# One raise for a chunk's twelve transposes and four activations, and a PSUM bank freed by its reader alone

## The chip, the cores and the metric

The program runs on one core of a Trainium2 chip. A core has five engines that run side by side, each an in-order queue: TensorE (PE in the profile, its weight loads PEld), VectorE (DVE), ScalarE (ACT), GpSimd (POOL) and SyncE (SP). They meet through semaphores: an instruction may wait until a semaphore has reached a value, and may raise one when it is done. DMA transfers raise semaphores when they land. The metric is the device time of one execution in microseconds; the median of 10 runs before is 7348.97 us (7343.96 to 7355.32).

## The reference

Two layers are applied to x, which has 4 images of 128 channels and 128 by 128 points.

```
x = x + deformable_conv(ln_c(x), w_off, w_conv)     # layer 0
t = tokens(x);  t = t + moe(ln_t(t))                # 8 experts, the best 2
x = x + fourier_mix(ln_c(x), alphas, betas)         # layer 1
t = tokens(x);  t = t + expert_choice(ln_t(t))      # 64 experts, 8 tokens each
```

The deformable convolution takes nine taps. For each tap and each output point a small convolution gives an offset; the input is read there by bilinear interpolation, which is a weighted sum of four neighbours; the nine samples of all channels go through w_conv. It is this sampling that the change touches: 4 images x 128 rows x 9 taps, each a gather of 128 points with four neighbours of 128 channels.

## The kernel before

**Tables and gathers.** Each image's normalised input is written to a table in DRAM whose entry holds two neighbouring rows' channels, so that one gathered stretch holds the four neighbours of a point. A *chunk* is one image row and three taps; there are 4 x 128 x 3 = 1536 chunks. Four rows make a group, and a group has twelve chunks: four rows with taps 0 to 2 (k0 = 0), then with 3 to 5, then with 6 to 8.

**A chunk's way** (class Chunk):

- `gather` (POOL): three indirect DMAs fill a tile g of 128 points x 3 taps x 4 neighbours x 128 channels. Seven such tiles are in turn (AHEAD), so the gather for chunk n + 7 reuses the tile of chunk n and waits until PE has read it.
- `weighted` (DVE): one multiplication with the interpolation weights, over all three taps when k0 = 0, over two taps otherwise.
- `weighted_too` (ACT), for k0 > 0: the third tap's four neighbours, one activation each, with the weight as its scale.
- `summed` (PE): a PSUM bank named trg; for each tap four transposes, one per neighbour, accumulate into the same 128 x 128, which sums the neighbours and turns channels to partitions. Twelve transposes in all.
- `moved` (ACT): one copy sT of the bank to SBUF. After the fourth row `convolved` multiplies sT with w_conv into the bank `sums` (PE).

**Everything else** is cut into coroutines (padding, offsets, block, mixed, experts, the last layer's Experts and Ending) that are resumed slot by slot. A slot is one chunk. The loop at the end of the function writes the order by hand: weighted of chunk n + 1, moved of chunk n - 2, one step of every coroutine, weighted_too of n + 1, summed of n, and then as many banks of the coroutines as there is room for (`Turns.fills`). `InOrder` keeps every engine's instructions in this order. Reading a bank comes two slots after its filling (`turns.hop` = 2).

**PSUM banks.** `bank` hands out six banks in turn (BANKS); two more are `sums` and `spread`. Fillings are groups of matmuls: four transposes (tr), one or four matmuls (pe, ps, pq, pl, po) or more. Readers are mostly one ACT copy of the whole bank; the experts' bank pe is read by one addition, or by four DVE instructions of a quarter each.

**Semaphores** are not written by hand. The framework records which instruction touches which tile and makes waits of it: a bank's new filling waits for all that touched its last content, thus for its readers and for PE's own earlier matmuls; a reader waits for the matmuls; a writer to g waits for the transposes. An instruction has room for one wait; what it needs beyond that goes into separate wait instructions ahead of it. Raises that nobody needs are folded into a later instruction of the same engine where the framework can do so: in the trace, 1,153 chunks have one raise on the twelfth transpose alone, and 383 chunks have five, on transposes 8 to 12, where transposes 9 to 12 each wait for one of the four activations.

All instructions are issued through the helper at line 101, so the profile shows L101 everywhere, and groups are told apart by their tiles.

Of the kernel before, what the change touches and what calls it, by code (L numbers as in the profile page):

```python
# [42 lines left out]
F32 = mybir.dt.float32  # L43
I32 = mybir.dt.int32
U32 = mybir.dt.uint32
AF = mybir.ActivationFunctionType
ALU = mybir.AluOpType
AX = mybir.AxisListType
PSUM = bass.MemoryType.PSUM
# [19 lines left out]
CB = 16  # L69
# [21 lines left out]
class InOrder:  # L91


    def __init__(self, tc, engine):
        self.tc, self.engine = tc, engine

    def __getattr__(self, name):
        issue = getattr(self.engine, name)

        def issued(*args, **kwargs):  # L100
            return self.tc.keep_in_program_order(issue(*args, **kwargs))  # L101

        return issued


class Engines:
    def __init__(self, tc):
        nc = tc.nc
        self.tensor, self.vector = InOrder(tc, nc.tensor), InOrder(tc, nc.vector)
        self.scalar, self.gpsimd = InOrder(tc, nc.scalar), InOrder(tc, nc.gpsimd)  # L110
        self.sync = InOrder(tc, nc.sync)


# [73 lines left out]
def metaformer_kernel(  # L187
# [16 lines left out]
    nc = tc.nc  # L204
# [6 lines left out]
    ident = const.tile([P, P], F32, name="ident")  # L211
# [26 lines left out]
    with ExitStack() as main:  # L238
# [7 lines left out]
        p_x = main.enter_context(tc.tile_pool(name="p_x", bufs=BANKS, space=PSUM))  # L246
# [2 lines left out]

        def bank(shape, name):  # L250

            return p_x.tile(shape, F32, name=name, tag="bank")

        eng = Engines(tc)
        turns = Turns()
# [4 lines left out]
        class Image:  # L260


            def __init__(self, b):
                self.b = b
                self.table = tabs.tile([TW * TC, 2 * P], F32, name=f"table{b}", tag="table")
                self.grid = self.table.rearrange("(i j) e -> i j e", j=TC)
                self.index = pw.tile([P, P, TAPS], I32, name=f"index{b}", tag="index")
                self.weight = {}
                self.xc = {}
                self.z = {}  # L270
                self.tails = {}


                self.read = self.normed = self.continued = self.sent = 0
                self.offsets = self.placed = self.known = 0
                self.left = 0
                self.direct = P // RB
                self.rooms = {}
# [91 lines left out]
        by = wts.tile([P, CB, TAPS], F32, name="by")  # L370
# [43 lines left out]
        def transposes(src, n, by=None):  # L414

            tr = bank([P, n, P], "tr")
            for i in range(n):
                if by is None:
                    eng.tensor.transpose(tr[:, i, :], src(i), ident)
                else:  # L420
                    eng.tensor.matmul(
                        tr[:, i, :], lhsT=src(i), rhs=by, is_transpose=True, start=True, stop=True
                    )
            return tr


# [2 lines left out]
        for w in [rw_sb] + [ew_sb[:, 4 * h : 4 * h + 4, :] for h in range(2)]:  # L429
            pw_c = bank(list(w.shape), "centred")  # L430
            eng.tensor.matmul(pw_c, lhsT=centre, rhs=w, start=True, stop=True)
            eng.scalar.copy(w, pw_c)


        def padding(t, h, row, read, padded):

            yield FILL
            tr = transposes(row, 4)
            read.append(h)
            yield turns.hop  # L440
            eng.scalar.copy(pads[(2 * t + h) % 4][:, :, 1 : P + 1], tr)
            padded.append(h)

        def offsets(im, t, padded):
# [5 lines left out]

            yield FILL
            po = bank([P, 4, P], "po")
            for k in range(3):
                for h in range(2):
# [52 lines left out]
        def block(im, t):  # L507
# [19 lines left out]
            def half(h):  # L527
                yield FILL
                tr = transposes(lambda i: xc[:, 4 * h + i, :], 4)
                im.read += 1  # L530
                yield turns.hop
# [197 lines left out]
        class Chunk:  # L729
# [28 lines left out]
            def weighted_too(self):  # L758
                g, y = self.g[:, 2], self.row.y
                w = self.row.group.im.weight[y // CB]  # L760
                for v in range(4):
                    eng.scalar.activation(
                        g[:, v, :], g[:, v, :], AF.Copy, scale=w[:, y % CB, self.k0 + 2, v : v + 1]
                    )

            def summed(self):

                self.tr = bank([P, 3, P], "trg")
                for i in range(3):
                    for v in range(4):  # L770
                        eng.tensor.matmul(
                            self.tr[:, i, :],
                            lhsT=self.g[:, i, v, :],
                            rhs=ident,
                            is_transpose=True,
                            start=(v == 0),
                            stop=(v == 3),
                        )

            def moved(self):  # L780
                group, s = self.row.group, self.row.s
                if s == 0:
                    group.sT = pb.tile([P, 3, 4, P], F32, name="sT", tag="sT")
                eng.scalar.copy(group.sT[:, :, s, :], self.tr)
                if s == 3:
                    turns.start(group.convolved(self.k0, group.sT))
# [4 lines left out]
        def mixed(group):  # L791
# [3 lines left out]
            yield 1  # L795
            yield FILL
            tr = transposes(lambda i: x1T[:, i, :], 4)
            yield turns.hop
            x1 = pb.tile([P, 4, P], F32, name="x1", tag="x1", bufs=4)
# [785 lines left out]
        start = turns.slot + 2  # L1585
# [126 lines left out]
```

## Time and profile before

| what | value |
|---|---|
| median of 10 runs | 7348.97 us |
| the profiled execution | 7351.38 us |
| its span, first to last instruction | 7349.4 us |
| mean granted TensorE clock | 0.896 |
| PE busy | 6011.7 us (82%) |
| DVE, POOL, ACT busy | 4792.5 (65%), 4420.3 (60%), 3706.6 us (50%) |
| sampling, first to last transposes of trg | 142 to 7134 us |
| PE's instructions that raise a semaphore | 6,022 |
| ACT's instructions that raise one | 6,256 |

The page's second part cuts the span into 40 slices; a digit is the busy share in tenths. In its fifth part each line is a group of instructions: line, engine, operation, output <- inputs, count, then busy time and the mean of one in ns, then the idle time of the engine before them and what ended most of it. In the list of waits a line is an engine, the tile it was about to write, and what ended the wait; then total us, times, and the longest. "Issue" stands for a wait that the profile can't explain, "remote" for a semaphore whose raising instruction had ended long before. In the timeline a line is start, duration, engine, instruction and count, with the idle time before it in brackets.

### The profile page before, as it was taken

What the parts mean: (1) busy time and instruction counts of PE and PEld (TensorE: products, weight loads), DVE (VectorE), ACT (ScalarE), POOL (GpSimd) and SP (SyncE); (2) the same over time, 40 slices, a digit from 0 to 9 for tenths busy, and PEclk for the clock granted to TensorE, in tenths of its full rate; (3) what the DMA queues carried; (4) which work ended last, traced back from release to release, by engine and by line L of the source; (5) the groups of instructions that cost most, each with busy time, mean ns of one, the idle gap of its engine ahead of it and who ended that gap; (6) DMA issues with size and microseconds to landing.
All of it is one profiled execution on the core that took longest, in us unless ns stands there. A gap on an engine that the chain in (4) does not pass through costs nothing. (4 is left out here: it accounts for less than half of the span.)

```text
span 7349.4 us, 103037 instructions
## 1 busy us (share of the span) xinstructions
PE 6011.7 (82%) x31271; PEld 3981.4 (54%) x31271; DVE 4792.5 (65%) x16100; ACT 3706.6 (50%) x9999; POOL 4420.3 (60%) x4691
## 2 busy tenths in 40 slices
PE   5788888888888888887888888888788788788885
PEld 3555555555555555555555555555555555565553
DVE  5466667676667666666667666667667665566663
ACT  4345555554555555554455555555444444444452
POOL 2666666666666666666666666666666665666641
PEclk8889999988889899998899989898888899899997
DMA  6666666666666666666666666666666677677777
GB/s 205 191 200 211 204 205 211 202 195 190 198 203 201 208 204 203 203 196 185 195 208 199 206 199 199 199 200 209 186 190 179 201 252 238 181 247 235 247 243 268
DMA packets 578917, 1524.69 MB, mean 207 GB/s; under 512 B 86424, under 2 KB 225408, under 8 KB 578368
## 3 DMA queue, kind: packets, MB, share of 16 engines
q0 software_dynamic: 369664, 1210.35, 55.0%
q1 hardware_dynamic: 206400, 299.36, 12.0%
q10 hardware_dynamic: 2304, 8.39, 0.3%
q8 instruction: 254, 4.16, 0.2%
q14 instruction: 295, 2.42, 0.1%
HBM read 1380.92 MB, written 136.85 MB: 207 GB/s over the span
## 5 line engine op out<-in xcount | busy, mean ns | idle before, releaser
L101 POOL DMA_INDIRECT g<-table,index x4608 | 4365.5, 947 | 2719.9 <-issue 1193.9
L101 PEld LDWEIGHTS trg<-ident,g 128*128 128x128 f32 x18432 | 2293.8, 149 | 1542.5 <-issue 1333.9
L101 PE MATMUL trg<-ident,g 128*128 128x128 f32 x18432 | 2580.7, 288 | 603.3 <-issue 521.4
L101 DVE SCALAR_TENSOR_TENSOR x<-pe,scaled,x 128x128 f32<-128x128 f32 x4048 | 1385.0, 342 | 1408.2 <-remote 642.4
L101 DVE TENSOR_TENSOR g<-g,spread 128x1024 f32<-128x1024 f32 (+1 forms) x1536 | 2130.5, 1388 | 201.1 <-ACT spread L101 108.6
L101 ACT COPY sT<-trg 128x384 f32<-128x384 f32 x1536 | 720.5, 471 | 2784.5 <-remote 1347.4
L101 PE MATMUL sums<-sT,wconv_sb 128*128 128x512 f32 x2304 | 1323.1, 656 | 50.3 <-issue 49.1
L101 ACT ACTIVATE g<-g,weight 128x128 f32<-128x128 f32 x4096 | 1306.3, 394 | 0.2
L101 PE MATMUL pe<-ew_sb,x1T 128*128 128x512 f32 x2048 | 1171.3, 653 | 125.0 <-issue 70.0
L101 PEld LDWEIGHTS sums<-sT,wconv_sb 128*128 128x128 f32 x2304 | 437.2, 209 | 523.8 <-issue 522.4
L101 PEld LDWEIGHTS pe<-ew_sb,x1T 128*128 128x128 f32 x2048 | 345.6, 206 | 233.6 <-issue 155.8
L101 ACT ACT_TABLE_LOAD x270 | 346.4, 1283 | 23.6 <-DVE nmax L101 10.2
L101 DVE TENSOR_TENSOR x<-ps,x 128x512 f32<-128x512 f32 x128 | 88.2, 689 | 268.2 <-remote 135.6
L101 PE MATMUL sums<-xg,ident 128*128 128x512 f32 x256 | 164.5, 729 | 114.9 <-ACT x1T L101 77.0
L101 PE MATMUL po<-pad,woff_sb 128*64 128x512 f32 x768 | 217.9, 644 | 26.8 <-issue 11.8
L101 DVE TENSOR_TENSOR x<-x,pe 128x512 f32<-128x512 f32 x128 | 87.1, 680 | 231.5 <-remote 132.4
L101 ACT ACTIVATE tn<-x,d_nb,d_rs 128x128 f32<-128x128 f32 x512 | 211.3, 488 | 7.9 <-DVE d_nb L101 2.9
L101 ACT ACTIVATE xn<-x,c_nb,c_rs 128x128 f32<-128x128 f32 x512 | 210.6, 485 | 6.0 <-DVE c_nb L101 4.5
L101 PE MATMUL pl<-rw_sb,x1T 128*128 128x8 f32 x1024 | 146.0, 260 | 68.3 <-issue 63.1
L101 PEld LDWEIGHTS pl<-rw_sb,x1T 128*128 128x128 f32 x1024 | 149.3, 217 | 69.6 <-issue 63.6
L101 ACT ACTIVATE ent<-raw,a_nb,a_rs 128x128 f32<-128x128 f32 x448 | 185.0, 485 | 3.3 <-DVE a_nb L101 2.8
L101 PE MATMUL pe<-eb_sb,gT 32*128 32x512 f32 x256 | 169.2, 743 | 16.8 <-issue 11.8
(227 smaller groups left out, 5143.4 us busy)
## 6 DMA issues: line engine op xcount, KB each, us to landing
g<-table,index POOLq DMA_INDIRECT x4608
table<-ent SPq DMA_DIRECT2D x64, 1024.0 KB
xc<-in_x SPq DMA_DIRECT2D x64, 512.0 KB
w<-x_d SPq DMA_DIRECT2D x64, 512.0 KB
xg<-in_x SPq DMA_DIRECT2D x124, 256.0 KB
x_d<-x SPq DMA_DIRECT2D x124, 256.0 KB
out<-w SPq DMA_DIRECT2D x48, 512.0 KB
w<-in_weight SPq DMA_DIRECT2D x40, 512.0 KB
```

The costliest lines, as they stand in the source:

```text
L101: return self.tc.keep_in_program_order(issue(*args, **kwargs))
```

## The change

Three things are done with the framework's record of dependences. It has groups: whoever would depend on a member of a group depends on the group's fence instead.

- `Batch`: a list of instructions of one engine; all but the last are members and the last is the fence. The twelve transposes of `summed` and the four activations of `weighted_too` become such batches.
- `Fills` and `Readers`: PE's instructions that write a bank are noted under the bank's name. When DVE, ACT or POOL issues an instruction that reads a noted bank, and the bank was filled by one instruction alone or the reader takes at least four fifths of it, the fillers become members of a group and that reader its fence. What came to wait for the fillers (a bank's new filling, a writer to the fillers' inputs) thus waits for the reader. The bank trg is left out; it has its batch.
- `transposes` calls matmul with is_transpose in both cases, where it called transpose in one.

```diff
+class Batch:
+    def add(self, made):
+        self.tc.add_to_no_dep_group(self.key, made.ins)
+        self.some = True
+    def end(self, made):
+        if self.some:
+            self.tc.declare_fence(made.ins, group=self.key)
+    def all(self, made):
+        for one in made[:-1]:
+            self.add(one)
+        self.end(made[-1])
...
+class Fills(InOrder):
+        def issued(*args, **kwargs):
+            made = issue(*args, **kwargs)
+            if args[0].name in self.sizes:
+                self.of.setdefault(args[0].name, []).append(made.ins)
+            return made
...
+class Readers(InOrder):
+        def issued(*args, **kwargs):
+            made = issue(*args, **kwargs)
+            for a in list(args) + list(kwargs.values()):
+                if isinstance(a, bass.AP) and a.space == PSUM and a.name in self.fills.of:
+                    filled = self.fills.of[a.name]
+                    if len(filled) == 1 or 5 * a.free_size() >= 4 * self.fills.sizes[a.name]:
+                        for ins in filled:
+                            self.tc.add_to_no_dep_group(a.name, ins)
+                        self.tc.declare_fence(made.ins, group=a.name)
+                        del self.fills.sizes[a.name], self.fills.of[a.name]
+                    break
+            return made
...
-            return p_x.tile(shape, F32, name=name, tag="bank")
+            tile = p_x.tile(shape, F32, name=name, tag="bank")
+            if name != "trg":
+                eng.tensor.sizes[tile.name] = tile.free_size()
+            return tile
...
-                for v in range(4):
-                    eng.scalar.activation(
-                        g[:, v, :], g[:, v, :], AF.Copy, scale=w[:, y % CB, self.k0 + 2, v : v + 1]
-                    )
+                Batch(tc).all(
+                    [
+                        eng.scalar.activation(
+                            g[:, v, :],
+                            g[:, v, :],
+                            AF.Copy,
+                            scale=w[:, y % CB, self.k0 + 2, v : v + 1],
+                        )
+                        for v in range(4)
+                    ]
+                )
...
                 self.tr = bank([P, 3, P], "trg")
-                for i in range(3):
-                    for v in range(4):
+                Batch(tc).all(
+                    [
                         eng.tensor.matmul(
                             self.tr[:, i, :],
                             lhsT=self.g[:, i, v, :],
...
+                        for i in range(3)
+                        for v in range(4)
+                    ]
+                )
```

More of the change, by code (lines that the diff above doesn't have):

```diff
@@ L103, in __getattr__, with __init__ @@
         return issued
+class Batch:
+    number = 0
+    def __init__(self, tc):
+        Batch.number += 1
+        self.tc, self.key, self.some = tc, f"batch{Batch.number}", False
+    def add(self, made):
[9 more added lines that the diff above has]
+class Fills(InOrder):
+    def __init__(self, tc, engine):
+        super().__init__(tc, engine)
+        self.sizes, self.of = {}, {}
+    def __getattr__(self, name):
+        issue = super().__getattr__(name)
+        def issued(*args, **kwargs):
[3 more added lines that the diff above has]
+            return made
+        return issued
+class Readers(InOrder):
+    def __init__(self, tc, engine, fills):
+        super().__init__(tc, engine)
+        self.fills = fills
+    def __getattr__(self, name):
+        issue = super().__getattr__(name)
+        def issued(*args, **kwargs):
[10 more added lines that the diff above has]
+            return made
+        return issued
 class Engines:
@@ L108, in __init__ @@
         nc = tc.nc
-        self.tensor, self.vector = InOrder(tc, nc.tensor), InOrder(tc, nc.vector)
-        self.scalar, self.gpsimd = InOrder(tc, nc.scalar), InOrder(tc, nc.gpsimd)
+        self.tensor = Fills(tc, nc.tensor)
+        self.vector, self.scalar, self.gpsimd = (
+            Readers(tc, engine, self.tensor) for engine in (nc.vector, nc.scalar, nc.gpsimd)
+        )
         self.sync = InOrder(tc, nc.sync)
@@ L417, in transposes @@
             for i in range(n):
[L418 to L422, printed above, removed]
-                    )
+                eng.tensor.matmul(
+                    tr[:, i, :],
+                    lhsT=src(i),
+                    rhs=ident if by is None else by,
+                    is_transpose=True,
+                    start=True,
+                    stop=True,
+                )
             return tr
@@ L760, in weighted_too @@
                 w = self.row.group.im.weight[y // CB]
-                for v in range(4):
-                    eng.scalar.activation(
-                        g[:, v, :], g[:, v, :], AF.Copy, scale=w[:, y % CB, self.k0 + 2, v : v + 1]
-                    )
+                Batch(tc).all(
[8 more added lines that the diff above has]
+                    ]
+                )
             def summed(self):
                 self.tr = bank([P, 3, P], "trg")
-                for i in range(3):
-                    for v in range(4):
+                Batch(tc).all(
+                    [
                         eng.tensor.matmul(
@@ L778, in summed @@
                         )
+                        for i in range(3)
+                        for v in range(4)
+                    ]
+                )
             def moved(self):
```

## The prediction

> **What bounds the kernel now.** I read the page first, then the list of waits, then the timeline of one stretch, and last the trace's records of semaphores. On the page:
>
> ```profile
> span 7349.4 us, 103037 instructions
> ...
> PE 6011.7 (82%) x31271; PEld 3981.4 (54%) x31271; DVE 4792.5 (65%) x16100; ACT 3706.6 (50%) x9999; POOL 4420.3 (60%) x4691
> ...
> PEclk8889999988889899998899989898888899899997
> ...
> L101 POOL DMA_INDIRECT g<-table,index x4608 | 4365.5, 947 | 2719.9 <-issue 1193.9
> L101 PE MATMUL trg<-ident,g 128*128 128x128 f32 x18432 | 2580.7, 288 | 603.3 <-issue 521.4
> L101 ACT COPY sT<-trg 128x384 f32<-128x384 f32 x1536 | 720.5, 471 | 2784.5 <-remote 1347.4
> L101 ACT ACTIVATE g<-g,weight 128x128 f32<-128x128 f32 x4096 | 1306.3, 394 | 0.2
> ```
>
> PE is the busiest engine, and a chunk takes (7134 - 142) / 1536 = 4.55 us from its first transpose to the next chunk's. But PE stands for 7349.4 - 6011.7 = 1338 us, and its clock is at half speed for 1526 us in 241 stretches (clock records). The readers of PSUM stand as well:
>
> ```profile
> ACT sT L101 <- remote: 1347.4, 295, 15.0
> PEld trg L101 <- issue: 1333.9, 2937, 3.6
> ...
> DVE x L101 <- remote: 910.3, 252, 16.0
> ...
> PE trg L101 <- issue: 521.4, 587, 3.1
> ...
> POOL g L101 <- remote: 366.8, 175, 4.7
> ```
>
> "Remote" on one core means that the semaphore moved long after the instruction that raises it. The columns are total us, times and longest. A stretch shows it:
>
> ```profile
> 3174.54 1.47 PE L101 MATMUL trg<-ident,g 128*128 128x128 f32 x12
> ...
> 3178.39 0.93 PE L101 MATMUL trg<-ident,g 128*128 128x128 f32 x7
> ...
> 3178.49 0.94 POOL L101 DMA_INDIRECT g<-table,index  x1 [0.30 <-issue]
> ...
> 3179.61 0.32 PE L101 MATMUL trg<-ident,g 128*128 128x128 f32 x1 [0.29 <-issue]
> ...
> 3181.03 0.27 PE L101 MATMUL trg<-ident,g 128*128 128x128 f32 x1 [1.10 <-issue]
> ...
> 3181.75 0.58 ACT L101 COPY pad<-tr 128x512 f32<-128x512 f32 x1 [4.34 <-PE trg L101]
> 3181.77 0.30 PE L101 MATMUL trg<-ident,g 128*128 128x128 f32 x1 [0.47 <-issue]
> ...
> 3183.86 0.37 PE L101 MATMUL trg<-ident,g 128*128 128x128 f32 x1 [1.80 <-issue]
> ```
>
> The first chunk's twelve transposes run 0.11 us apart; transposes 8 to 12 each raise PE's semaphore. Matched in order, those five raises arrive at 3176.71, 3181.73, 3185.34, 3185.37 and 3185.41, though the last transpose started at 3175.75. ACT stands for them, and soon PE itself takes one transpose per 0.7 or 1.4 us though nothing is awaited. Over the trace (5,435 of 6,022 raises have a record) a raise arrives a median 3.2 us after its matmul starts. Queued raises mostly follow each other within 80 ns (1,898 times; POOL's gathers ran 9% of that time) or after 0.6 us and more (1,036 times; gathers ran 56 to 69%). So PE's raises leave one by one, and slowly while gathers are issued. ACT's recorded raises come 9 ns after their instruction.
>
> **The change, part by part.** (a) Raises of the transposes. By the semaphores in the instruction records, 1,153 chunks carry one raise on PE already (earlier ones are folded into the last) and 383 carry five; these are the chunks whose last four transposes each wait for ACT. Copy and gather need only the last, so 383 x 4 = 1,532 of 6,022 go (25%). Where a raise and the one before it are both on record, the time that it stood at the head of the queue can be taken: 1,134 of the 1,532 stood 726 us, 0.64 us each, and all raises 4,540 us. So these have 16% of the queue's time, and 1,532 x 0.64 = 980 us in all.
>
> The Trainium skill ("TensorE: Matmul & The Clock Gate", "The cost: per-tile semaphore tail") holds that raises of matmuls serialize at 26.3 ns each and that one on the last matmul is sound. By that price (a) would be worth an estimated 40 us at most, near the short spacing here; the long one, 0.6 us and more, it does not know.
>
> What of the 980 us is on the path? First, PE's stalls: 614 times a load and its matmul stand about 0.70 us apart with no wait, 430 us; in 135 the raise next to arrive is one of the 1,532: 135 x 0.70 = 95 us. The lower bound is 0 (the next raise takes its place at the head), the upper is all 430. I take 95, what was counted.
>
> Second, PE's idle time behind late readers. The rows of PE and its loads that end with ACT or DVE (sums behind x1T 110.3 and 77.0; trg, pe, tr behind sT 70.2, 57.5, 45.1, 32.0, 28.7, 26.3; smaller ones) overlap; the time itself is about 250 us. With 16% less queue: 40 us. Bounds 0 and 250.
>
> Third, the clock. Half speed for 1526 us, with PE busy 82%, costs about 1526 x 0.82 / 2 = 620 us, and the stretches follow lulls of PE. 95 + 40 = 135 us of 1338 us less is 10%; 10% of 620 is 62. I take 50, since the clock's stretches are multiples of 3.41 us in the records and short lulls need not matter; bounds 0 and 120.
>
> (b) Four activations, one raise: 1,149 fewer raises on ACT. Spacing of such activations is 293 ns with a raise and 292 without: nothing. But the ninth transpose now waits for the fourth activation, not the first. The late case before ends four transposes as "last activation + 0.11 us", after it as "+ 0.44 us": 0.33 us lost. In 110 of the 383 the last four transposes were late at all: at most 36 us; the row of loads that waited for such an activation has 55 cases (20.1 us): 18 us at least. I take 24. Behind the waiting ninth stands all of PE's queue; ACT's copy and POOL's next gather wait for the twelfth.
>
> (c) The reader frees the bank. A new filling waits for the reader alone, not for PE's own earlier raise as well. PE has 923 waits on its own semaphore; as enders of PE's idle time they come to 1.0 us, since the reader had waited for the same raise. So 0; an upper bound is some 500 separate wait instructions of 51 ns, 25 us, which run ahead beside matmuls. For the experts' bank the first of four readers takes PE's place; the other three still hold the bank. Inputs of such a filling are free when the reader is done, not the matmul: SP's loads into xc and the experts' weights start up to one copy (0.6 us) later, and all behind them in SP's queue. They run a block ahead, so nothing; if that cover went, 64 loads x 0.6 = 38 us. (d) transpose written as matmul: the same instruction, 0.
>
> Sum: 95 + 40 + 50 - 24 = 161 us. The profiled execution took 7351.4, 2.0 over its span; 7351.4 - 161 = 7190, and the median of the runs shown is 2.4 below that execution: 7188.
>
> The skill's "VectorE: DVE Perf Modes" ("The DRAIN you can't avoid") speaks against thinning raises for speed: it measured none gained on DVE. It would set (b)'s raises to zero, as ACT's 292 against 293 ns does here.
>
> **The rivals.**
>
> *The queue pays in full.* If standing raises pace PE, ACT and POOL together, part of the 980 us comes straight off: 40% is 390 us, 6959. For it: "remote" rows of 1347, 910 and 367 us. Against: PE's own stalls behind these raises are 95 us.
>
> *Hidden anyway.* If the queue opens when gathers end and not by count, the raise that is left stands as long as five did. For it: the extra raises' median time at the head is 42 ns; most leave in a row. Groups of twelve chunks with more five-raise chunks are not longer in the first three images (-0.1 +- 0.3 us a chunk). Gain 10 to 30 us: 7330.
>
> *Slower by the ninth transpose.* It waits for the fourth activation, and if PE comes closer behind ACT than now, each of the 1,024 chunks with activations can lose 0.33 us: 338 us. It decides from 161 / 0.33 = 490 late chunks; before, 110 + 96 were late. With 800 late and half of the gain gone: 264 - 80 = 184, 7533; just past the point, 7365. For it: PE gets faster and ACT does not. Against: activations are issued a whole chunk (4.55 us) ahead.
>
> *No change in the raises:* should the transposes keep five, 7349.
>
> **How the numbers follow.** Forecast 0.52 (own range 7090 to 7310), queue in full 0.14, hidden or no change 0.16 (half of it within 0.2%), ninth transpose 0.18. The measurement tells 0.2% (15 us) from no change. Faster 0.52 + 0.14 + 0.08 = 0.74, same 0.08, slower 0.18. The range leaves out the lower half of the second case (0.07) and the slower case beyond 7400 (0.11): 6930 to 7400.
>
> **What would show it.** Right: raises on PE near 4,490; PE's load row for trg behind "issue" under 1,200 us, ACT's and DVE's "remote" rows down by a fifth, fewer half-clock stretches. (b) shows as the row of trg behind ACT's g, 20.1 us now, growing by some 20 us. (c) shows as PE without waits on itself, at no change elsewhere. Wrong, if raises fall and "remote" does not (hidden), if trg behind ACT's g passes 200 us (ninth transpose), or if the banks are handed out in another order and another engine's wait grows.

## The result and the profile after

The changed kernel takes 7385.73 us (median of 8 runs, 7375.90 to 7392.89) against 7349.51 us of the kernel before (28 runs): a ratio of 1.0048, 95% interval 1.0039 to 1.0057. It is 36 us slower; 161 us of gain were forecast. The page of the profiled execution after:

```profile
span 7381.4 us, 103049 instructions
...
PE 6021.1 (82%) x31271; PEld 3991.7 (54%) x31271; DVE 4791.5 (65%) x16100; ACT 3706.3 (50%) x9999; POOL 4422.1 (60%) x4691
...
PEclk8889999988899889898889989898888899889897
...
L101 POOL DMA_INDIRECT g<-table,index x4608 | 4367.3, 948 | 2739.6 <-issue 1244.5
...
L101 PE MATMUL trg<-ident,g 128*128 128x128 f32 x18432 | 2584.6, 289 | 591.6 <-issue 497.5
...
L101 ACT COPY sT<-trg 128x384 f32<-128x384 f32 x1536 | 719.5, 472 | 2740.8 <-remote 1383.4
...
L101 ACT ACTIVATE g<-g,weight 128x128 f32<-128x128 f32 x4096 | 1306.4, 394 | 0.4
```

The span grew by 32.0 us: PE's busy time by 9.4, its idle time by 22.6. All other engines do the same work in the same time. PE's raises fell as forecast, from 6,022 to 4,495, one per chunk for the transposes. The list of waits shows that nothing came of it:

```profile
ACT sT L101 <- remote: 1383.4, 293, 14.9
PEld trg L101 <- issue: 1304.2, 2879, 4.0
...
DVE x L101 <- remote: 983.0, 245, 13.3
...
POOL g L101 <- ACT sT L101: 549.9, 235, 7.4
...
PE trg L101 <- issue: 497.5, 576, 2.9
...
POOL g L101 <- remote: 210.4, 97, 4.6
```

ACT's row behind late raises stands at 1383 us where it was 1347, DVE's at 983 where it was 910. A raise arrives a median 3.06 us after its matmul starts (3.20 before). The clock records show half speed for 1603 us in 251 stretches, where it was 1526 us in 241. One row grew that the prediction never spoke of, POOL's gathers behind ACT. Before, it read:

```profile
POOL g L101 <- ACT sT L101: 364.7, 160, 6.7
```

That row is 185 us longer. Much of this is a change of name: POOL's row behind late raises fell by 156 us, from 366.8 to 210.4, and the page's idle time ahead of all gathers grew by 20 us, from 2719.9 to 2739.6. The name also misleads: no gather waits for sT. By the wait values, every gather that waits for ACT waits for the fourth activation of the chunk that last used its tile, seven chunks back, and PE's transposes waited for that activation too. The copy sT and the gather are both released by the same raise of PE, that of the twelfth transpose. So the timeline can be read with the copy as a clock. Two places of the kernel *before*, where POOL stood idle and copy and gather waited for the same raise:

```profile
2204.97 0.48 ACT L101 COPY sT<-trg 128x384 f32<-128x384 f32 x1 [2.67 <-PE trg L101]
...
2205.68 0.95 POOL L101 DMA_INDIRECT g<-table,index  x1 [1.98 <-ACT sT L101]
...
2443.55 0.48 ACT L101 COPY sT<-trg 128x384 f32<-128x384 f32 x1 [3.32 <-PE tr L101]
...
2443.78 0.94 POOL L101 DMA_INDIRECT g<-table,index  x1 [1.74 <-PE tr L101]
```

Once the gather starts 0.71 us after the copy, once 0.23 us. The instruction records tell the two apart. An instruction carries one wait; further ones sit in wait instructions ahead of it. In the second place the gather carries the wait for PE itself, and the wait instruction ahead holds older conditions. In the first the gather carries the wait for ACT, met long before, and the wait for PE sits in the instruction ahead. From raise to start it is 259 ns in the first form and 728 ns in the second, in the median over all such places and within a few ns in every trace here: 469 ns apart. The same after:

```profile
2481.32 0.48 ACT L101 COPY sT<-trg 128x384 f32<-128x384 f32 x1 [3.63 <-remote]
...
2482.03 0.94 POOL L101 DMA_INDIRECT g<-table,index  x1 [2.82 <-ACT sT L101]
```

Before, of the 1,017 chunks with activations whose tile is reused, 636 had the slow form and 381 the fast one. The fast ones are exactly the five-raise chunks, in which the twelfth transpose itself waited for the fourth activation. With the change only the ninth waits, and all 1,017 gathers are in the slow form. Gathers that start from a standing POOL in that form (over 1.6 us after the gather before) went from 266 to 379.

### The profile page after: what moved, and what is told of

Read it like the earlier page. It is cut to its first block, busy times and chain, and to the rows that moved or that the text cites. A ratio compares the mean times of both kernels' runs of the same rounds, so it can differ in the third digit from the quotient of the medians.

```text
span 7381.4 us, 103049 instructions
## 1 busy us (share of the span) xinstructions
PE 6021.1 (82%) x31271; PEld 3991.7 (54%) x31271; DVE 4791.5 (65%) x16100; ACT 3706.3 (50%) x9999; POOL 4422.1 (60%) x4691
## 5 line engine op out<-in xcount | busy, mean ns | idle before, releaser
L101 POOL DMA_INDIRECT g<-table,index x4608 | 4367.3, 948 | 2739.6 <-issue 1244.5
```

## The experiments

Runs of one group share a chip, on which the kernel before took 7278.0 us (first four), 7274.3 (next four) and 7282.9 (last two); ratios are what can be compared. The table counts gathers that wait for ACT; the expectations count 12 waits of other POOL instructions with them (1,029 for 1,017, 648 for 636), so 13 such waits are left where they say 0. In e5 and e10 the chunks with five raises are 380, not 383.

| run | gathers' waits for ACT | PE's raises | median us | ratio to before, interval |
|---|---|---|---|---|
| e1 activations alone | 1,017 | 4,490 | 7303.39 | 1.0037, 1.0023 to 1.0051 |
| e2 banks alone | 636 | 6,027 | 7287.75 | 1.0009, 1.0000 to 1.0019 |
| e3 ninth waits, gathers not for ACT | 0 | 4,489 | 7211.76 | 0.9913, 0.9900 to 0.9927 |
| e4 gathers not for ACT | 0 | 6,021 | 7217.91 | 0.9918, 0.9905 to 0.9932 |
| e5 gathers not for DVE | 639 | 5,993 | 7276.11 | 1.0000, 0.9991 to 1.0009 |
| e6 whole change, gathers not for ACT | 0 | 4,494 | 7220.24 | 0.9921, 0.9907 to 0.9934 |
| e7 gathers for PE alone, ninth waits | 0 | 4,472 | 7200.35 | 0.9893, 0.9878 to 0.9908 |
| e8 one gather of three | 636 | 5,844 | 5381.29 | one run, two of three taps not sampled |
| e9 transposes alone | 636 | 6,022 | 7283.88 | 1.0001, 0.9992 to 1.0010 |
| e10 as e7, five raises | 0 | 5,992 | 7210.43 | 0.9901, 0.9886 to 0.9916 |

**e1, e2, e9: one part of the change at a time.** The theories were: the ninth transpose's later wait (A), POOL's added waits (B), the banks (C).

```diff
 e1: the kernel before, and in weighted_too
+                Batch(tc).all([eng.scalar.activation(...) for v in range(4)])
 e2: the kernel before with Fills and Readers
 e9: the kernel before, and in summed
+                Batch(tc).all([eng.tensor.matmul(...) for i in range(3) for v in range(4)])
```

> Only the four activations are a batch; transposes and banks as before. By the kernels' instructions this alone takes the five raises of 383 chunks' transposes to one (PE's raises 6,022 to 4,490), lets the ninth transpose wait for the fourth activation in these chunks, and gives POOL 381 more separate wait instructions ahead of gathers (waits on ACT 648 to 1,029). Theory A, the ninth transpose costs: about the whole loss, 7380 to 7390 us, and PE's loads of trg behind ACT longer than before in these chunks. Theory B, POOL's added waits cost (36 us / 381 = 95 ns each): 7380 to 7390 too, with POOL's gaps ahead of a chunk's first gather longer by about 0.1 us in those chunks. Theory C, the banks cost: 7349 or less. Theory D, nothing of it but fewer raises: 7340 to 7349.

> Only the banks are freed by their readers; transposes and activations as before (PE's waits on itself 923 to 222, PE's separate wait instructions 2,614 to 2,215, raises 6,027). Theories A and B: 7345 to 7352 us, no change. Theory C, a bank freed by its reader moves loads or hands a bank over later: 7380 to 7390, all of the loss here.

> Only the batch of the twelve transposes (and transposes of banks written as matmuls); activations and banks as before. By its instructions every wait and raise is as before: 6,022 raises on PE, 383 chunks with five. So all theories: ratio 0.999 to 1.001. If the batch of transposes did something by itself after all, the raises in the trace are fewer than 6,022.

The activations' batch alone loses 25 us, and it alone takes PE's raises to 4,490, as the whole change does (4,495). The transposes' batch does nothing: 6,022 raises on PE in its trace, ratio 1.0001. The five raises hang on the waits of transposes 9 to 12; once only the ninth waits, the framework folds them into the twelfth by itself. The banks are at +10 us, with an interval from nothing to 14.

**e3, e4: take the gathers' waits for ACT away.** The activations become members of a group whose fence is the twelfth transpose, which follows them anyway. In e3 the ninth transpose gets an explicit dependence on the fourth activation, as in the change.

```diff
 e4, in summed (self.writers holds the chunk's four activations, made its transposes)
+                Batch(tc).all(self.writers + made[-1:])
 e3, besides
+                if self.writers:
+                    tc.add_manual_dep(made[8].ins, self.writers[3].ins.name, ...)
```

> Banks and transposes as before. The ninth transpose is made to wait for the fourth activation as in the change (PE's raises 4,489), but the gathers no longer wait for ACT at all (1,029 to 0 waits on ACT; POOL's separate wait instructions 2,594 to 1,581): the twelfth transpose stands for the activations, which it follows anyway. Theory A, the ninth transpose costs: about 7385 us, as the change. Theory B, POOL's waits cost 95 ns each: 1,029 fewer than in the change, 7385 - 98 = 7287. Theory C: 7349.

> As before (five raises in 383 chunks, 6,021 on PE, each transpose waits for its own activation), but no gather waits for ACT (648 to 0; POOL's separate wait instructions 2,214 to 1,581). Theory A: 7349 us. Theory B, 95 ns each: 7349 - 62 = 7287. Theory C: 7349. If both A and B hold in part, the difference of this to the run with the ninth transpose is A's share, and its difference to the kernel before B's.

Both come out 60 to 66 us *below* the kernel before. The waits for ACT cost 60 us in the kernel before (e4 to before: 636 of them, 94 ns each) and 92 us in e1 (e3 to e1: 1,017, 90 ns each). Theory B's price was 95 ns. Theory A falls: e3 has the later ninth transpose just as e1 has, and is 92 us faster. Against e4, e3 has the later ninth transpose and 1,532 fewer raises together, and is 6 us faster, less than the measurement resolves. No run takes these two apart, but the rows of PE behind the activations show that the ninth transpose costs something, in e4 first, then in e3:

```profile
PEld trg L101 <- ACT g L101: 20.4, 67, 2.2
...
PE trg L101 <- ACT g L101: 4.2, 6, 2.0
```

```profile
PEld trg L101 <- ACT g L101: 46.5, 51, 3.2
...
PE trg L101 <- ACT g L101: 28.6, 27, 2.9
```

They grew by 26 and 24 us. If both reached the end in full, the fewer raises alone would be worth some 55 us; if neither did, 6. The list of waits of e1, then of e3, for POOL and the copy:

```profile
ACT sT L101 <- remote: 1452.4, 303, 16.3
...
POOL g L101 <- ACT sT L101: 521.7, 237, 6.6
...
POOL g L101 <- remote: 241.0, 111, 4.5
```

```profile
ACT sT L101 <- remote: 1083.6, 309, 15.1
...
POOL g L101 <- remote: 514.6, 281, 4.5
```

POOL's row behind ACT is gone from e3; part of it now stands as remote, which names the raise that the gather does wait for. In e3's timeline the gather follows the copy by 0.24 us:

```profile
2395.41 0.48 ACT L101 COPY sT<-trg 128x384 f32<-128x384 f32 x1 [5.97 <-PE trg L101]
...
2395.65 0.94 POOL L101 DMA_INDIRECT g<-table,index  x1 [1.57 <-PE trg L101]
```

In e1, 349 gathers start from a standing POOL in the slow form: 349 x 0.469 = 164 us of POOL's time. If the whole difference of 92 us comes from them, some 56% of it reaches the end. The span falls from 7304.8 to 7207.8 us; of these 97.0 us, 43.0 are PE's busy time (granted clock 0.897 to 0.912) and 54.0 its idle time.

**e5: the number of wait instructions, or the place of one wait?** e4 removes both 633 wait instructions and the slow form. e5 makes the twelfth transpose stand for DVE's multiplication instead: as many wait instructions go (624), and the slow form stays.

```diff
+                self.writers = [eng.vector.tensor_tensor(gf, gf, ...)]
...
+                Batch(tc).all(self.writers + made[-1:])
```

> As before (five raises in 383 chunks, ninth transpose unchanged), but the gathers no longer wait for DVE's multiplication (1,537 to 0), for which the twelfth transpose stands; they still wait for ACT in 651 chunks. So POOL's separate wait instructions fall from 2,214 to 1,590, as in the run without waits on ACT (1,581), but in the 651 chunks the wait for PE still sits in the separate instruction ahead and the gather itself waits for ACT. Theory B1, each separate wait instruction costs: ratio to before 0.992, as without waits on ACT. Theory B2, the place of the wait for PE costs (a gather starts 728 ns after PE's raise where that wait stands in a separate instruction and 259 ns where the gather itself carries it, by the traces of all runs so far): ratio 0.998 to 1.002, and 728 ns in the trace for these chunks.

The ratio is 1.0000, and the slow form still takes 728 ns from raise to start. In its timeline:

```profile
2494.35 0.48 ACT L101 COPY sT<-trg 128x384 f32<-128x384 f32 x1 [2.18 <-PE trg L101]
2495.05 0.95 POOL L101 DMA_INDIRECT g<-table,index  x1 [1.50 <-ACT gT L101]
```

So wait instructions whose conditions are long met cost nothing that shows; what costs is that the wait that is met last sits in one of them. Every slow gather here carries a wait for ACT in its place; whether one for another engine would do the same was not tried.

**e6, e7: the change repaired, and a faster version.**

```diff
 e6: e3 with Fills and Readers
 e7: e3 with all writers of g in the group
+                    self.writers.append(eng.gpsimd.indirect_dma_start(...))
...
+                self.writers.append(eng.vector.tensor_tensor(gf, gf, ...))
```

> The whole change (banks freed by readers, ninth transpose waits for the fourth activation, 4,494 raises on PE) without any wait of the gathers for ACT (1,029 to 0). If the waits on POOL are the change's main loss, its ratio goes from 1.005 to that of the run with the ninth transpose and no such wait, 0.991, plus the banks' share, 0.0009: 0.992. If the change loses by anything else as well, it stays above 0.994.

> Banks as before, ninth transpose waits for the fourth activation (4,472 raises on PE), and the twelfth transpose stands for all writers of g, the gathers, the multiplication and the activations: the next gather waits for PE alone, beside the wait of its DMA queue (separate wait instructions on POOL 1,584, ACT's 478 instead of 1,354). Theory B2, the place of the wait for PE: ratio 0.991, no better than without the waits on ACT. If the other waits, met long before, cost as well: 0.985 or less.

The whole change without the gathers' waits for ACT goes from 1.0048 to 0.9921, the value worked out ahead. e7 beats both kernels and is the fastest here, 74 us below the kernel before. Its lead over e3, 0.0020 and from another group of runs, is no larger than the uncertainty of that difference, so whether the other waits, met long before, cost a little as well is not settled.

**e10: fewer raises, a second time.**

```diff
 e7 without
-                    tc.add_manual_dep(made[8].ins, self.writers[-1].ins.name, ...)
```

> As the run in which the next gather waits for PE alone (0.9893), but transposes 9 to 12 each wait for their own activation as before: five raises in 383 chunks (5,992 on PE instead of 4,472). A second measure of fewer raises and a later ninth transpose together. By the prediction's sum (161 us net): 7200 + 161, ratio 1.011 relative to 0.9893, so 1.000 to before. By the first measure (6 us): 0.990. If the later ninth transpose cost as much as its rival said, this would be under 0.985.

0.9901 against e7's 0.9893 on another chip: again some 6 us for 1,520 fewer raises and a later ninth transpose together, and again less than the two intervals resolve.

**e8: are PE's raises held up by the gathers?**

```diff
-                for i in range(3):
+                eng.sync.dma_start(out=self.g[:, 1:3], in_=<the table's first 512 rows>)
+                for i in range(1):
                     eng.gpsimd.indirect_dma_start(...)
```

> Leaves out two of three gathers: taps two and three of a chunk come by one plain load on SP's queue, of the same size but of the table's first rows, so the sampled values are wrong; all else as before. POOL's gathers fall from 4,608 to 1,536. If PE's raises stand because of the gathers on POOL (the prediction's reading), the median from a matmul's start to its raise falls from 3.2 to under 1 us, ACT's time behind remote raises from 1347 to under 500 us, although the raises are as many (5,844 against 6,022). If they stand for PE's own reasons or for the traffic, which stays, the median stays above 2.5 us.

Lines of the page of e8, and after them one of its list of waits:

```profile
span 5378.3 us, 104639 instructions
...
PE 5203.3 (97%) x31271; PEld 3630.1 (67%) x31271; DVE 4749.5 (88%) x16100; ACT 3726.4 (69%) x9999; POOL 1512.7 (28%) x1619
...
PEclk8999999999999999999999999999999999999997
```

```profile
ACT sT L101 <- remote: 2.5, 2, 1.6
```

With a third of the gathers, about the same number of raises and the same 1,524.7 MB moved, a raise arrives a median 0.29 us after its matmul starts instead of 3.2 us, ACT's remote row falls to 2.5 us, and PE is busy 97% of the time at full clock nearly throughout. What holds PE's raises is the gathers, not how many raises there are. Which part of a gather does it, POOL's work on it or its many small transfers, this run does not tell.

## Why the prediction was wrong

The forecast of 7188 us missed in sign; the range, 6930 to 7400, holds 7386 by luck, since its slow side stood for the ninth transpose, which is not what cost the time.

- **(a), raises of the transposes, 95 + 40 + 50 us.** The count was right (1,532 go), the worth was not. e3 against e4 and e7 against e10 give 6 us each, with the ninth transpose's later wait in it, and without that wait some 55 us at most by the rows of e3 and e4, not 185. The step that failed is "So these have 16% of the queue's time", taken as time that goes with them. In e4 the transposes' raises stood 2,927 us at the head of the queue (2,627 of 3,068 on record), in e3, with half of these raises gone, 3,418 us (1,410 of 1,536 on record); taken up to all raises, that is about 3,420 and 3,720 us. The standing did not fall; the one raise that is left stands longer, 2.4 us each. That was the "hidden anyway" rival, whose sign ("raises fall and remote does not") is what the trace shows. Its 10 to 30 us were nearer than the forecast. From the kernel before to the changed one, whose gathers differ in form, the time in which any raise of PE stood did fall, by some 8% as an estimate (5.1 to 4.7 ms, raises matched to the waits that they end), and the kernel lost all the same.
- **(b), the ninth transpose, -24 us, and its rival.** PE's loads of trg behind ACT's g went from 20.1 to 26.9 us, PE's own from 3.9 to 14.9, and in e3 against e4 they grew by 26 and 24 us: one to two times the price, and far from 200 us. The rival that ended on the slow side is not what happened.
- **(b), what it left out.** "Copy and gather need only the last" looked at when the twelfth transpose's raise comes, and not at how the gather waits for it. Taking the waits from transposes 10 to 12 moved 381 gathers into the slow form. The row for this was in the trace of before: 266 of 636 gathers of that form started from a standing POOL, so 381 x 266 / 636 = 159 more of them x 0.469 = 75 us of POOL's time; with 56% of it on the path, 42 us. Measured by e1: 25 us, with the net gain of 6 us from fewer raises and the later ninth transpose in it, thus about 31. The sum has no such term; this one, with the banks, turned the sign.
- **(c), banks, 0 with a bound of 38 us.** +10 us, 0 to 14 (e2). PE's waits on itself fell from 923 to 222 as named. Whether these 10 us are the loads on SP that start later, or nothing, was not settled.
- **(d)** is nothing, as said (e9 has it too).
- **What bounds the kernel.** PE is the busiest engine, but e8 shows that its clock, its standing and its late raises follow from the gathers. A loss on POOL's way from raise to gather therefore counts, though POOL is busy 60%.

The two halves of the change, measured by themselves, give 25 (e1) + 10 (e2) = 35 us; the change lost 36.

The Trainium skill's "TensorE: Matmul & The Clock Gate" ("The cost: per-tile semaphore tail") would have 1,532 raises at 26.3 ns each worth an estimated 40 us. The runs show 6 us with the ninth transpose's wait in it and leave room for up to some 55 without it, so they do not decide whether that price holds here.

The skill's "Perfetto Trace Analysis" ("DMA Instruction — SWDGE (GPSIMD)") draws a DMA of POOL as decoded and pushed into a wait queue before its semaphores are met. That agrees with the fast form, 259 ns from raise to start, if the decoding of a gather behind a wait instruction comes after the wait; the page gives no time for this, and the runs give the difference, 469 ns, and not its cause.

## What to carry to other kernels

When a change thins waits or raises, list for each consumer which wait its instruction carries itself and which go into wait instructions ahead: on POOL, the wait that is met last belongs on the gather. A fence on the consumer's own last releaser (here the twelfth transpose for every writer of g) removes the waits that are met anyway and puts the right one in place, for 1.1% here. Before pricing a queue by how long its entries stand, ask what opens it: if that is another engine's activity, fewer entries can stand longer.

## What the runs showed of the hardware

- A gather whose wait for PE sits in a wait instruction ahead, while it carries one for ACT, starts 728 ns after the raise; one that carries the wait for PE starts after 259 ns. On ACT the same difference is small: copies that carry the wait for PE start 23 ns after the raise (some 830 cases after the change), copies with it in an instruction ahead 77 ns (49 copies sT before it).
- Gathers from a full queue start one every 1.25 us, 0.30 us after the last one's end, whatever their form: the slow form costs only where POOL had been standing.
- PE's raises arrive a median 3.2 us after their matmul with three gathers a chunk and 0.29 us with one; the granted clock is 0.896 and 0.987.
